# Filler products on TensorE ahead of seven waits, and twice as many behind one transpose, in a two-layer feed-forward kernel

## The chip, the cores and the metric

The kernel runs on one core of a Trainium2 chip. The metric is the device time of one execution in microseconds (us). Engines are named as in the profile: PE is TensorE (PEld its weight loads), DVE VectorE, ACT ScalarE, POOL GpSimd, SP SyncE, which here issues almost all DMAs.

## What is computed

The reference adds two feed-forward layers to x (8 sequences of 512 tokens, 256 features), each fed by a conditioning step chosen by an integer per sequence. The first layer is a quantised FFN: its input and its hidden activation h are rounded to 8 bits with one scale for the whole tensor, so nothing behind h can be quantised before the largest |h| of all tokens is known. The second layer sends each token to the best two of nine experts.

```python
def _L0_ffn_ref(x, clip_x, clip_down, w_gate, w_up, w_down):
    def _act_fake_quant(x, clip_factor):
        scale = jax.nn.sigmoid(clip_factor) * jnp.max(jnp.abs(x)) / QMAX
        return jnp.clip(_ste_round(x / scale), -QMAX - 1.0, QMAX) * scale
    ...
    h = _act_fake_quant(jax.nn.silu(gate) * up, clip_down[0])
    return jnp.einsum('bsi,hi->bsh', h, _weight_fake_quant(w_down))
...
def _L1_ffn_ref(x, Wr, Wg, Wu, Wd):
    ...
    topk_w, topk_idx = jax.lax.top_k(probs, TOP_K)
    ...
    gate = jax.nn.silu(jnp.einsum('th,ehi->tei', xf, Wg))
    hidden = gate * jnp.einsum('th,ehi->tei', xf, Wu)
    out = jnp.einsum('tei,eih,te->th', hidden, Wd, cw)
...
x = x + _L0_ffn_ref(_L0_cond_ref(x, ...), ...)
x = x + _L1_ffn_ref(_L1_cond_ref(x, ...), ...)
```

## The kernel before

The program has three stages, each one straight line of instructions.

The **front** conditions x, quantises it and computes h. Its steps are small functions (`gp`, `up` products of gate and up weights; `sl`, `st`, `uc`, `pm` activation and product; `mx` the largest |h| of a chunk, line 519 is `st`, 316 the reduction of `mx`). The text `FRONT` lists them in the order in which they are issued. A step `z_n` (lines 331 to 335) issues n matrix products of a tile of zeros, `busy`, into the PSUM bank that the next step will use; nobody reads them. There are four such banks, `wide0` to `wide3`, handed out in turn. After `FRONT` come lines 538 to 546: the largest |h| per partition (`htop_own`, line 539), a transpose on TensorE into the next bank (line 320), `z(ZEROS_BEHIND)`, that is 12 products of zeros, and then, on DVE, the maximum over all partitions and the scale of h.

The **middle** is listed in `ORDER`, again in the order of issue, one name for each piece with its batch (0 to 7) or block number. For each batch: `qa` and `qd` quantise h (ACT, then a clip on DVE), `dp` multiplies by the down weights and `dv` adds to x; `ap`, `aa`, `xp`, `xa`, `zp`, `zv` run the second conditioning step (`xs` stores x by SP), `np`, `nv`, `na`, `nw` its layer norm; `tp` transposes the normed rows back (`ta` copies them), `cp`, `ce`, `ct`, `cv`, `ca` choose the experts, `hp` and `hv` find each token's place in the expert's list, and `hg` scatters the rows into those lists in DRAM: eight indirect DMAs for each batch, on the POOL queue (line 880). `pp` and `pw` plan which blocks of 128 list rows come next.

Mixed in, and then alone in the **tail**, are blocks of 128 rows for one expert each: `R` fetches the rows, `U` and `W` the expert's weights if they change (all SP's queue), `t` transposes the rows on DVE, `g..a`, `g..b`, `g..c` are the gate and up products (line 1098), `va` to `vd` the activation, `d` the down product (line 1146), `y` the weighting and `s` the scatter into the output (POOL, line 1156). `ORDER` carries 14 blocks; the rest, up to 72, are issued by a loop.

Every engine takes its instructions in the order of issue and waits where a semaphore says so. In the middle there are six PSUM banks `bank0` to `bank5` handed out in turn, and two more, `tok0` and `tok1`, for `xp` and `zp`.

Of the kernel before, what the change touches and what calls it, by code (L numbers as in the profile page):

```python
# [32 lines left out]
P = 128  # L33
# [17 lines left out]
    up_2_3 mx_2_1 sl_2_3 up_2_4 mx_1_3 uc_2_3 up_3_0 st_2_4 gp_2_5 uc_3_0 pm_2_3 gp_3_0 mx_2_4 sl_2_5 up_2_5 up_3_1  # L51
    sl_3_0 st_2_5 gp_3_2 mx_2_5 uc_3_1 pm_3_0 mx_2_2 gp_3_1 sl_3_2 up_3_2 mx_2_3 sl_3_1 up_3_4 st_3_2 gp_3_5 pm_3_1
    uc_3_4 up_3_3 mx_3_0 sl_3_5 gp_3_4 mx_3_2 gp_3_3 sl_3_4 mx_3_1 up_3_5 sl_3_3 pm_3_4 st_3_5 st_3_3 mx_3_3 mx_3_4
    mx_3_5
"""
LAST_LOAD = "L_dT"
ZEROS_BEHIND = 12
ORDER = """
    qa0d fa1 fa0 fa2 qa0b qd0d qa0a qd0b qa0c fg0 fg1 qd0a qa2b qd0c dp0b qa1b qa1a dp0a qd1b dv0b qd1a dv0a dp1b
    qd2b qa2a xp0_1 dv1b xp0_0 ap0 xa0_1 qd2a xa0_0 dp1a qa2c xs0 aa0 qd2c qa4a zp0_0 dv1a zp0_1 zv0_0 qa3b ap1 fa3  # L60
    zv0_1 qa3a dp2a qd3b np0 aa1 qd3a dp2b dv2a pu1 pd0 nv0 dp3a dv2b na0_1 qd4a pu2 na0_0 nw0_1 xp1_1 ap2 qa4c
    xa1_1 nw0_0 xp1_0 qa4b zp1_1 dv3a xa1_0 tp0_0 pu0 aa2 zv1_1 zp1_0 ta0_0 qd4b tp0_1 qa5b zv1_0 dp3b ta0_1 qd4c
    np1 qa6b cp0 dv3b xs1 dp4b qd5b ce0 qa5a nv1 fa4 ct0 ap3 dv4b na1_1 mz0 cv0 dp4a na1_0 qa6c pd2 xp2_0 aa3 pd1
    xp2_1 nw1_1 hp0 ca0 fg2 xa2_1 hv0 tp1_1 xa2_0 zp2_1 ta1_1 xs2 nw1_0 hg0_0 zp2_0 zv2_1 tp1_0 fa5 ta1_0 zv2_0
    hg0_2 cp1 qd5a ce1 dv4a ct1 fg3 cv1 dp5b hg0_1 ap4 qd6b ca1 hp1 dv5b np2 aa4 dp5a hv1 qa6a hg0_3 nv2 pp0a qa7a
    pw0a dv5a pp0b pw0b na2_1 ap5 hg1_1 qd6a na2_0 pp0c qd6c nw2_1 dp6b qa7b hg1_3 nw2_0 xp3_1 xp3_0 xa3_1 pw0c fg4
    tp2_0 xa3_0 zp3_1 ta2_0 hg1_2 dv6b xs3 tp2_1 zv3_1 zp3_0 ta2_1 U0 qd7b cp2 aa5 zv3_0 hg1_0 ce2 fa6 dp6a qd7a
    ct2 dp7a dv6a np3 cv2 U1 dp7b W1 ap6 nv3 ca2 R0 dv7b na3_1 hp2 dv7a na3_0 xp4_0 hv2 xa4_0 xp4_1 nw3_0 R1 zp4_0
    xa4_1 zp4_1 nw3_1 tp3_0 aa6 t0 tp3_1 ta3_0 zv4_1 g0a W0 ta3_1 xs4 w0 zv4_0 fa7 cp3 va0 t1 hg2_1 g0b ce3 w1 fg5
    ct3 g0c vb0 np4 cv3 U2 g1a vc0 hg2_0 W2 nv4 g1b ca3 U3 vd0 va1 na4_1 hg2_2 g1c vb1 na4_0 nw4_1 d0 vc1 U4 hg2_3  # L70
    nw4_0 vd1 tp4_1 y0 xp5_0 ta4_1 s0 xp5_1 xa5_0 tp4_0 xa5_1 fg6 zp5_0 ta4_0 zp5_1 zv5_0 W3 cp4 zv5_1 ap7 ce4 R2
    ct4 np5 hp3 aa7 cv4 xs5 hv3 ca4 R3 nv5 hp4 hv4 na5_0 na5_1 t2 xp6_1 R4 w2 g2a xa6_1 nw5_0 nw5_1 tp5_0 va2 zp6_1
    ta5_0 t3 R5 d1 w3 zv6_1 t4 w4 tp5_1 y1 R6 xp6_0 ta5_1 s1 g2b xa6_0 zp6_0 vb2 W4 cp5 zv6_0 R7 g2c ce5 np6 g3a t5
    vc2 w5 nv6 vd2 ct5 xs6 na6_0 g3b U5 cv5 na6_1 d2 va3 fg7 hg3_3 nw6_1 ca5 nw6_0 hp5 W5 hg3_1 tp6_1 g3c hv5 ta6_1
    y2 tp6_0 vc3 U6 t6 xp7_0 hg4_0 ta6_0 w6 xp7_1 vb3 xa7_0 xa7_1 vd3 zp7_0 pp1a hg5_3 zv7_0 cp6 g4a ce6 pw1a xs7
    hg4_1 pp1b va4 g4b pw1b pp1c vb4 hg3_0 g4c pw1c d3 t7 vc4 U7 w7 hg3_2 vd4 g5a y3 W6 s2 d4 va5 hg4_3 g5b y4 W7
    s3 g5c vb5 hg4_2 g6a vc5 U8 vd5 hg5_2 g6b va6 g6c vb6 hg5_0 d5 vc6 U9 vd6 hg5_1 zp7_1 y5 ct6 W8 g7a zv7_1 s4
    cv6 d6 np7 va7 R8 nv7 ca6 na7_0 g7b s5 y6 na7_1 nw7_0 R9 hp6 g7c hv6 tp7_0 nw7_1 vc7 s6 ta7_0 R10 t8 tp7_1 w8
    g8a vb7 ta7_1 vd7 t9 d7 va8 w9 U10 R11 g8b y7 t10 s7 w10 cp7 vb8 g8c ce7 R12 ct7 g9a vc8 cv7 g9b va9 W10 t11
    ca7 U11 vd8 g9c w11 vb9 hg6_2 W9 d8 t12 vc9 w12 vd9 U12 hg6_1 g10a y8 W11 g10b s8 va10 hg6_3 g10c vb10 d9 vc10  # L80
    U13 vd10 hg6_0 g11a y9 W12 s9 d10 va11 R13 g11b y10 s10 g11c vb11 R14 g12a vc11 vd11 t13 d11 va12 w13 U14 R15
    g12b t14 y11 s11 g12c vb12 W14 hp7 vc12 R16 g13a hv7 vd12 pp2a va13 g13b pw2a R17 pp2b vb13 d12 pw2b W13 pp2c
    y12 U15 g13c pw2c s12 W15 vc13 hg7_3 U16 vd13 hg7_0 hg7_1 hg7_2
"""
BLOCKS_IN_ORDER = 14

# [2 lines left out]
def adaln_ffn_kernel(  # L89
# [21 lines left out]
    nc = tc.nc  # L111

    B, _, KC, S = xT.shape
# [21 lines left out]
    def act_scale(top, sig, name):  # L135
# [27 lines left out]
    start = rt.tile([P, NJ, E], F32, name="start")  # L163
    nc.gpsimd.iota(
        start, pattern=[[0, NJ], [CAP, E]], base=0, channel_multiplier=0, allow_small_or_imprecise_dtypes=True
# [13 lines left out]
    wdT = l0.tile([P, NM, D], BF16, name="wdT")  # L179
# [26 lines left out]
    turn_of = {}  # L206
# [35 lines left out]
    with tc.tile_pool(name="hw", bufs=1) as hw, tc.tile_pool(  # L242
# [75 lines left out]
        def across(pi, col, n, i):  # L318

            nc.tensor.transpose(pi[:, i : i + n], col.to_broadcast([n, P]), ident[:n, :n])  # L320
# [9 lines left out]
        @front  # L330
        def z(n):

            pz = wide_sb[(turn_of.get("wide", -1) + 1) % len(wide_sb)]
            for _ in range(n):
                nc.tensor.matmul(pz[:, :S], lhsT=busy[:, :P], rhs=busy, start=True, stop=True)
# [205 lines left out]
        across(ph, own, P, 0)  # L541
        z(ZEROS_BEHIND)
        htop = l0.tile([P, 1], F32, name="htop")
# [8 lines left out]
    banks_sb = [psum.tile([P, 512], F32, name=f"bank{k}") for k in range(6)]  # L552
# [615 lines left out]


    @piece  # L1170
    def pu(i, k):
        rows_of = slice(LIKELY[i] * P, (LIKELY[i] + 1) * P)
        nc.sync.dma_start(gu_sb[i].rearrange("p c n -> p (c n)"), Wx[rows_of, : KC * GU])
# [147 lines left out]
```

## Time and profile before

| | |
|---|---|
| median of 6 runs | 726.46 us (725.04 to 731.04) |
| profiled execution, its own time | 727.25 us |
| its span, first to last instruction | 725.5 us |
| mean granted TensorE clock | 0.971 |
| PE busy | 672.7 us, 93% |
| PE LDWEIGHTS busy | 569.6 us, 79% |
| DVE, ACT, POOL busy | 337.9, 202.3, 207.4 us |
| products of zeros (line 335) | 19.0 us, 55 recorded |
| longest single waits of PE | 5.3 us (line 320, for `htop_own`), 4.4 us (line 963, for `leap`), 2.8 us (line 1098, for the transposed rows) |

The page divides the span into 40 slices of 18.1 us and gives for each the busy share of every engine in tenths and the granted TensorE clock:

```profile
PE   9989798778787899999999999999999999999995
PEclk9999899898898999999999999999999999999998
DMA  8600049456377966323265532389825488225742
```

A 9 stands for 90% or more. In the fifth to the fourteenth slice (72 to 254 us) several slices have a granted clock below 0.9 and a TensorE that is idle for a tenth to three tenths of the slice; from the fifteenth on TensorE is busy for 90% or more of each slice, at a clock of 0.9 or more in all but the last. A single place is read from stretches that are cut finer than these slices, and from the instructions in order of time.

### The profile page before, as it was taken

What the parts mean: (1) busy time and instruction counts of PE and PEld (TensorE: products, weight loads), DVE (VectorE), ACT (ScalarE), POOL (GpSimd) and SP (SyncE); (2) the same over time, 40 slices, a digit from 0 to 9 for tenths busy, and PEclk for the clock granted to TensorE, in tenths of its full rate; (3) what the DMA queues carried; (4) which work ended last, traced back from release to release, by engine and by line L of the source; (5) the groups of instructions that cost most, each with busy time, mean ns of one, the idle gap of its engine ahead of it and who ended that gap; (6) DMA issues with size and microseconds to landing.
All of it is one profiled execution on the core that took longest, in us unless ns stands there. A gap on an engine that the chain in (4) does not pass through costs nothing. (4 is left out here: it accounts for less than half of the span.)

```text
span 725.5 us, 14632 instructions
## 1 busy us (share of the span) xinstructions
PE 672.7 (93%) x4678; PEld 569.6 (79%) x4688; DVE 337.9 (47%) x1036; ACT 202.3 (28%) x407; POOL 207.4 (29%) x190
## 2 busy tenths in 40 slices
PE   9989798778787899999999999999999999999995
PEld 3333254448676789899999999999999999999994
DVE  3989778674763164333333333333333333333331
ACT  4698686533330121111111111111111111111110
POOL 1036304715155535352121212212121121212212
PEclk9999899898898999999999999999999999999998
DMA  8600049456377966323265532389825488225742
GB/s 344 208 8 1 1 147 373 151 175 216 78 226 223 303 188 199 63 73 51 47 194 150 156 55 46 52 254 339 251 32 123 118 287 235 34 45 150 236 86 32
DMA packets 86641, 107.91 MB, mean 149 GB/s; under 512 B 58904, under 2 KB 75424, under 8 KB 82976
## 3 DMA queue, kind: packets, MB, share of 16 engines
q1 hardware_dynamic: 73696, 89.61, 39.6%
q0 software_dynamic: 12720, 17.31, 12.4%
q8 instruction: 39, 0.64, 0.3%
q14 instruction: 42, 0.34, 0.2%
q10 hardware_dynamic: 144, 0.01, 0.0%
HBM read 183.55 MB, written 22.83 MB: 284 GB/s over the span
## 5 line engine op out<-in xcount | busy, mean ns | idle before, releaser
L1098 PE MATMUL bank<-upper__104,lower 128*128 128x128 f32 x2636 | 316.4, 278 | 12.0 <-issue 9.1
L1098 PEld LDWEIGHTS bank<-upper__104,lower 128*128 128x128 f32 x2636 | 311.2, 194 | 17.9 <-issue 11.4
L1156 POOL DMA_INDIRECT out_dram<-upper__104,tag x67 | 104.1, 1553 | 366.7 <-DVE upper__104 L1088 281.9
L1114 DVE TENSOR_TENSOR upper__104<-bank,upper__104 128x512 f32<-128x512 f32 x67 | 46.3, 691 | 170.6 <-PE bank L1098 147.7
L1108 ACT ACTIVATE upper__104<-bank 128x512 f32<-128x512 f32 x67 | 40.1, 598 | 246.0 <-PE bank L1098 198.2
L880 POOL DMA_INDIRECT lists<-row,sloti x64 | 64.0, 1001 | 49.6 <-issue 16.9
L1146 PE MATMUL bank<-upper__104 128*128 128x256 f32 x312 | 72.4, 382 | 0.0
L1146 PEld LDWEIGHTS bank<-upper__104 128*128 128x128 f32 x312 | 58.0, 193 | 7.0
L1146 PE MATMUL tok<-upper__104 128*128 128x256 f32 x216 | 49.6, 379 | 0.0
L1146 PE MATMUL bank<-lower,upper__104 128*128 128x256 f32 x180 | 43.5, 393 | 0.2 <-issue 0.2
L1146 PEld LDWEIGHTS tok<-upper__104 128*128 128x128 f32 x216 | 39.7, 190 | 4.6
L1124 ACT ACTIVATE upper__104<-bank 128x128 f32<-128x128 f32 x41 | 11.4, 278 | 111.7 <-PE bank L1098 106.4
L1152 DVE TENSOR_SCALAR upper__104<-bank,wt 128x256 f32<-128x256 f32 x41 | 19.8, 484 | 44.6 <-PE bank L1146 40.6
L1098 PE MATMUL tok<-upper__104,lower 128*128 128x128 f32 x312 | 39.1, 275 | 0.0
L1146 PEld LDWEIGHTS bank<-lower,upper__104 128*128 128x128 f32 x180 | 34.7, 200 | 5.6 <-issue 1.1
L1098 PEld LDWEIGHTS tok<-upper__104,lower 128*128 128x128 f32 x312 | 36.9, 192 | 0.0
L1130 DVE TENSOR_TENSOR upper__104<-bank,upper__104 128x128 f32<-128x128 f32 x41 | 11.9, 290 | 43.8 <-ACT upper__104 L1125 35.8
L1124 ACT ACTIVATE upper__104<-tok 128x128 f32<-128x128 f32 x26 | 7.2, 278 | 63.9 <-PE tok L1098 63.9
L506 ACT ACTIVATE g<-wide,swg 128x1024 f32<-128x1024 f32 (+1 forms) x24 | 24.1, 1041 | 3.1 <-PE wide L482 2.4
L1152 DVE TENSOR_SCALAR upper__104<-tok,wt 128x256 f32<-128x256 f32 x26 | 12.6, 484 | 21.4 <-PE tok L1146 21.4
L640 PE MATMUL bank<-yq,wdT 128*128 128x512 bf16 x75 | 20.4, 396 | 1.9 <-ACT ha L678 1.2
L1130 DVE TENSOR_TENSOR upper__104<-tok,upper__104 128x128 f32<-128x128 f32 x26 | 7.6, 292 | 31.3 <-ACT upper__104 L1125 31.3
(215 smaller groups left out, 707.1 us busy)
## 6 DMA issues: line engine op xcount, KB each, us to landing
lower<-in_L_ffn_W_dram SPq DMA_DIRECT2D x73, 1408.0 KB
upper__104<-in_L_ffn_W_dram SPq DMA_DIRECT2D x48, 768.0 KB
lower<-in_L_ffn_W_dram SPq DMA_DIRECT2D x24, 768.0 KB
lower<-lists SPq DMA_DIRECT2D x144, 32.0 KB
upper__104<-lists SPq DMA_DIRECT2D x140, 32.0 KB
x_sb<-in_x_dram SPq DMA_DIRECT2D x8, 512.0 KB
out_dram<-xtok SPq DMA_DIRECT2D x8, 512.0 KB
lists<-pad SPq DMA_DIRECT2D x10, 130.0 KB
```

The source lines that it names most:

```text
L506: nc.scalar.activation(g, pg, AF.Silu, scale=swg[:, m : m + 1])
L640: nc.tensor.matmul(pd, lhsT=wdT[:, m, cs], rhs=hq_sb[b % 2][:, m], start=m == 0, stop=False)
L880: nc.gpsimd.indirect_dma_start(out=own_rows[(b * NJ + j) * 2 + n], out_offset=bass.IndirectOffsetOnAxis(ap=sloti_sb[b % 3][:, j, n : n + 1 ...
L1098: nc.tensor.matmul(pg[:, at * P : (at + 1) * P], lhsT=gu_sb[i % NW][:, c, n * P : (n + 1) * P], rhs=xbT_sb[i % 3][:, c], start=c == 0, sto ...
L1108: nc.scalar.activation(g_sb[i % 3][:, :4].rearrange("p m t -> p (m t)"), held.pop(("pg", i, "a")), AF.Silu)
L1114: nc.vector.tensor_tensor(hid_sb[i % 3][:, :4].rearrange("p m t -> p (m t)"), held.pop(("pg", i, "b")), g_sb[i % 3][:, :4].rearrange("p m ...
L1124: nc.scalar.activation(gs[:, 4], pg[:, :P], AF.Silu)
L1130: nc.vector.tensor_tensor(hid[:, 4], pg[:, P : 2 * P], gs[:, 4], ALU.mult)
L1146: nc.tensor.matmul(po[:, :D], lhsT=hid_sb[i % 3][:, m], rhs=dn_sb[i % NW][:, m], start=m == 0, stop=m == NM - 1)
L1152: nc.vector.tensor_scalar(y_sb[i % 3], held.pop(("po", i))[:, :D], small_["wt"][i % NX], None, ALU.mult)
L1156: nc.gpsimd.indirect_dma_start(out=out, out_offset=bass.IndirectOffsetOnAxis(ap=tag_sb[i % NX][:, 0:1].bitcast(I32), axis=0), in_=y_sb[i % 3],
```

## The change

Filler products are added at seven places, and the number behind the transpose of h's maximum goes from 12 to 24. In the front the existing step `z` is used: `z_22` at the end of `FRONT`, ahead of the transpose. In the middle a new piece `zz` issues n products of the down weights with themselves (128x512 bf16) into the bank that the next piece will take, and nothing reads them. `zz5` stands between `pp0a` and `pp0b`, `zz10` ahead of `g0a`, `zz8` ahead of `hp4`, `zz4` behind `t2` and ahead of `xp6_1`, `zz24` ahead of `tp7_0`, `zz6` ahead of `tp7_1`. Otherwise `ORDER` keeps its sequence; its lines are only broken elsewhere.

```diff
     uc_3_4 up_3_3 mx_3_0 sl_3_5 gp_3_4 mx_3_2 gp_3_3 sl_3_4 mx_3_1 up_3_5 sl_3_3 pm_3_4 st_3_5 st_3_3 mx_3_3 mx_3_4
-    mx_3_5
+    mx_3_5 z_22
 """
 LAST_LOAD = "L_dT"
-ZEROS_BEHIND = 12
+ZEROS_BEHIND = 24
 ORDER = """
...
-    ... pp0a qa7a pw0a dv5a pp0b pw0b ...
+    ... pp0a qa7a pw0a dv5a zz5 pp0b pw0b ...
-    ... tp3_1 ta3_0 zv4_1 g0a W0 ...
+    ... tp3_1 ta3_0 zv4_1 zz10 g0a W0 ...
-    ... R3 nv5 hp4 hv4 na5_0 na5_1 t2 xp6_1 ...
+    ... R3 nv5 zz8 hp4 hv4 na5_0 na5_1 t2 zz4 xp6_1 ...
-    ... hp6 g7c hv6 tp7_0 nw7_1 vc7 s6 ta7_0 R10 t8 tp7_1 ...
+    ... hp6 g7c hv6 zz24 tp7_0 nw7_1 vc7 s6 ta7_0 R10 t8 zz6 tp7_1 ...
...
     @piece
+    def zz(n, k):
+
+        pz = banks_sb[(turn_of.get("bank", -1) + 1) % len(banks_sb)]
+        for _ in range(n):
+            nc.tensor.matmul(pz, lhsT=wdT[:, 0, :P], rhs=wdT[:, :2].rearrange("p m d -> p (m d)"), start=True, stop=True)
+
+    @piece
     def pu(i, k):
```

That is 91 products more on PE: 34 with zeros and 57 with the down weights. The instructions of ACT, POOL and SP and their order stay as they are. On DVE one instruction changes its place: the memset of the small tile `half` (line 591), which stands ahead of the fourth clip of h in the kernel before, stands behind it in the changed kernel. The first product of `z_22` carries a wait for DVE, the one that frees its bank; the products of `zz` carry no wait of their own.

More of the change, by code (lines that the diff above doesn't have):

```diff
@@ L53 @@
     uc_3_4 up_3_3 mx_3_0 sl_3_5 gp_3_4 mx_3_2 gp_3_3 sl_3_4 mx_3_1 up_3_5 sl_3_3 pm_3_4 st_3_5 st_3_3 mx_3_3 mx_3_4
-    mx_3_5
+    mx_3_5 z_22
 """
 LAST_LOAD = "L_dT"
-ZEROS_BEHIND = 12
+ZEROS_BEHIND = 24
 ORDER = """
[L59 to L83, printed above, removed]
@@ new lines @@
+    qa0d fa1 fa0 fa2 qa0b qd0d qa0a qd0b qa0c fg0 fg1 qd0a qa2b qd0c dp0b qa1b qa1a dp0a qd1b dv0b qd1a dv0a dp1b qd2b
+    qa2a xp0_1 dv1b xp0_0 ap0 xa0_1 qd2a xa0_0 dp1a qa2c xs0 aa0 qd2c qa4a zp0_0 dv1a zp0_1 zv0_0 qa3b ap1 fa3 zv0_1
+    qa3a dp2a qd3b np0 aa1 qd3a dp2b dv2a pu1 pd0 nv0 dp3a dv2b na0_1 qd4a pu2 na0_0 nw0_1 xp1_1 ap2 qa4c xa1_1 nw0_0
+    xp1_0 qa4b zp1_1 dv3a xa1_0 tp0_0 pu0 aa2 zv1_1 zp1_0 ta0_0 qd4b tp0_1 qa5b zv1_0 dp3b ta0_1 qd4c np1 qa6b cp0 dv3b
+    xs1 dp4b qd5b ce0 qa5a nv1 fa4 ct0 ap3 dv4b na1_1 mz0 cv0 dp4a na1_0 qa6c pd2 xp2_0 aa3 pd1 xp2_1 nw1_1 hp0 ca0 fg2
@@ new lines @@
+    xa2_1 hv0 tp1_1 xa2_0 zp2_1 ta1_1 xs2 nw1_0 hg0_0 zp2_0 zv2_1 tp1_0 fa5 ta1_0 zv2_0 hg0_2 cp1 qd5a ce1 dv4a ct1 fg3
+    cv1 dp5b hg0_1 ap4 qd6b ca1 hp1 dv5b np2 aa4 dp5a hv1 qa6a hg0_3 nv2 pp0a qa7a pw0a dv5a zz5 pp0b pw0b na2_1 ap5
+    hg1_1 qd6a na2_0 pp0c qd6c nw2_1 dp6b qa7b hg1_3 nw2_0 xp3_1 xp3_0 xa3_1 pw0c fg4 tp2_0 xa3_0 zp3_1 ta2_0 hg1_2
+    dv6b xs3 tp2_1 zv3_1 zp3_0 ta2_1 U0 qd7b cp2 aa5 zv3_0 hg1_0 ce2 fa6 dp6a qd7a ct2 dp7a dv6a np3 cv2 U1 dp7b W1 ap6
+    nv3 ca2 R0 dv7b na3_1 hp2 dv7a na3_0 xp4_0 hv2 xa4_0 xp4_1 nw3_0 R1 zp4_0 xa4_1 zp4_1 nw3_1 tp3_0 aa6 t0 tp3_1
@@ new lines @@
+    ta3_0 zv4_1 zz10 g0a W0 ta3_1 xs4 w0 zv4_0 fa7 cp3 va0 t1 hg2_1 g0b ce3 w1 fg5 ct3 g0c vb0 np4 cv3 U2 g1a vc0 hg2_0
+    W2 nv4 g1b ca3 U3 vd0 va1 na4_1 hg2_2 g1c vb1 na4_0 nw4_1 d0 vc1 U4 hg2_3 nw4_0 vd1 tp4_1 y0 xp5_0 ta4_1 s0 xp5_1
+    xa5_0 tp4_0 xa5_1 fg6 zp5_0 ta4_0 zp5_1 zv5_0 W3 cp4 zv5_1 ap7 ce4 R2 ct4 np5 hp3 aa7 cv4 xs5 hv3 ca4 R3 nv5 zz8
+    hp4 hv4 na5_0 na5_1 t2 zz4 xp6_1 R4 w2 g2a xa6_1 nw5_0 nw5_1 tp5_0 va2 zp6_1 ta5_0 t3 R5 d1 w3 zv6_1 t4 w4 tp5_1 y1
+    R6 xp6_0 ta5_1 s1 g2b xa6_0 zp6_0 vb2 W4 cp5 zv6_0 R7 g2c ce5 np6 g3a t5 vc2 w5 nv6 vd2 ct5 xs6 na6_0 g3b U5 cv5
@@ new lines @@
+    na6_1 d2 va3 fg7 hg3_3 nw6_1 ca5 nw6_0 hp5 W5 hg3_1 tp6_1 g3c hv5 ta6_1 y2 tp6_0 vc3 U6 t6 xp7_0 hg4_0 ta6_0 w6
+    xp7_1 vb3 xa7_0 xa7_1 vd3 zp7_0 pp1a hg5_3 zv7_0 cp6 g4a ce6 pw1a xs7 hg4_1 pp1b va4 g4b pw1b pp1c vb4 hg3_0 g4c
+    pw1c d3 t7 vc4 U7 w7 hg3_2 vd4 g5a y3 W6 s2 d4 va5 hg4_3 g5b y4 W7 s3 g5c vb5 hg4_2 g6a vc5 U8 vd5 hg5_2 g6b va6
+    g6c vb6 hg5_0 d5 vc6 U9 vd6 hg5_1 zp7_1 y5 ct6 W8 g7a zv7_1 s4 cv6 d6 np7 va7 R8 nv7 ca6 na7_0 g7b s5 y6 na7_1
+    nw7_0 R9 hp6 g7c hv6 zz24 tp7_0 nw7_1 vc7 s6 ta7_0 R10 t8 zz6 tp7_1 w8 g8a vb7 ta7_1 vd7 t9 d7 va8 w9 U10 R11 g8b
@@ L84 @@
+    y7 t10 s7 w10 cp7 vb8 g8c ce7 R12 ct7 g9a vc8 cv7 g9b va9 W10 t11 ca7 U11 vd8 g9c w11 vb9 hg6_2 W9 d8 t12 vc9 w12
+    vd9 U12 hg6_1 g10a y8 W11 g10b s8 va10 hg6_3 g10c vb10 d9 vc10 U13 vd10 hg6_0 g11a y9 W12 s9 d10 va11 R13 g11b y10
+    s10 g11c vb11 R14 g12a vc11 vd11 t13 d11 va12 w13 U14 R15 g12b t14 y11 s11 g12c vb12 W14 hp7 vc12 R16 g13a hv7 vd12
+    pp2a va13 g13b pw2a R17 pp2b vb13 d12 pw2b W13 pp2c y12 U15 g13c pw2c s12 W15 vc13 hg7_3 U16 vd13 hg7_0 hg7_1 hg7_2
 """
```

## The prediction

> **What bounds the kernel now.** I read the page's 40 slices, then busy time by stretches, then TensorE's order of time with its waits, then the other engines beside each wait. From 295 us on TensorE has work without a break, so whatever time it wins or loses before that reaches the end one for one. Before 295 us it waits in many places, and a granted clock of 0.50 follows some waits. The stretches, each cut at an edge of the clock's record or at the ends of a wait (columns: stretch, length, busy us and count of PE, PEld, DVE, ACT, POOL, then granted clock, DMA share, GB/s):
>
> ```profile
> 78.40:83.73 5.33, 0.01 (x2) 0.01 (x2) 5.20 (x7) 0.75 (x1) 2.17 (x1) 0.87 0.00 0
> 82.30:89.13 6.83, 5.40 (x13) 2.04 (x14) 3.28 (x10) 4.06 (x5) 0.00 (x0) 0.50 0.00 0
> 123.26:126.67 3.41, 1.75 (x8) 0.79 (x11) 2.23 (x13) 0.27 (x1) 2.80 (x3) 1.00 1.08 372
> 130.08:133.50 3.42, 1.30 (x11) 0.66 (x11) 3.11 (x17) 3.38 (x4) 2.81 (x3) 1.00 0.42 143
> 133.50:140.33 6.83, 6.83 (x26) 4.48 (x25) 4.84 (x17) 4.46 (x8) 5.30 (x6) 0.50 0.39 131
> 160.80:164.22 3.42, 3.42 (x28) 2.78 (x28) 2.49 (x12) 0.60 (x1) 1.63 (x2) 0.50 0.71 209
> 171.04:174.46 3.42, 1.68 (x12) 1.47 (x12) 0.00 (x0) 0.00 (x0) 2.04 (x3) 1.00 0.87 216
> 184.70:188.11 3.41, 0.35 (x8) 0.20 (x6) 3.02 (x22) 1.15 (x6) 1.03 (x1) 1.00 0.66 181
> 188.11:194.94 6.83, 5.29 (x33) 5.20 (x33) 5.89 (x23) 2.83 (x6) 0.00 (x0) 0.50 0.27 46
> 295.00:705.00 410.00, 408.88 (x3069) 391.53 (x3068) 144.03 (x451) 62.42 (x164) 91.91 (x63) 1.00 0.53 135
> ```
>
> All clock edges lie on a grid of 3.41 us. A cell of it in which TensorE was busy 1.68 us or less (0.49) is followed by half clock, one with 1.75 us (0.51) is not. Half clock lasts one or two cells. Seven stretches of it stand before 295 us; the change fills waits ahead of four: 82.30, 133.50, 160.80, 188.11.
>
> TensorE's own order around the edits (start, length, line, what, count, [idle before it and what ended it]):
>
> ```profile
> 83.73 0.48 PE L320 MATMUL wide<-ident,htop_own 128*128 128x128 f32 x1 [5.32 <-DVE htop_own L539]
> 84.00 5.29 PE L335 MATMUL wide<-busy 128*128 128x512 bf16 x12
> 89.34 1.24 PE L640 MATMUL bank<-yq,wdT 128*128 128x512 bf16 x4
> ...
> 159.96 1.34 PE L1098 MATMUL bank<-upper__104,lower 128*128 128x128 f32 x8 [2.81 <-DVE upper__104 L1088]
> ...
> 262.20 1.58 PE L1098 MATMUL bank<-upper__104,lower 128*128 128x128 f32 x12
> 263.62 0.60 PE L776 MATMUL bank<-ident,row 128*128 128x128 f32 x4
> 265.25 0.63 PE L776 MATMUL bank<-ident,row 128*128 128x128 f32 x4 [1.03 <-issue]
> 265.72 1.95 PE L1098 MATMUL bank<-upper__104,lower 128*128 128x128 f32 x16
> ```
>
> The reader should see that tp7_0 at 263.62 follows g7c (262.20) with no wait at all; the largest filler, 24 products, goes between those two.
>
> Price of one filler: 8 products of the same form (L482, 128x512 bf16) take 1.89 us at full clock, so 0.216 us each; at half clock 12 take 5.29 us, so 0.43 us.
>
> **z_22 and 24 instead of 12.** The first product writes the bank that st_3_3 reads last, so it waits for the second of these two:
>
> ```profile
> 78.54 1.94 DVE L519 SCALAR_TENSOR_TENSOR upper__104<-wide,swu,g 128x512 f32<-128x512 f32 x2
> 80.52 2.94 DVE L316 TENSOR_REDUCE hmax<-upper__104 128x1 f32<-128x1024 f32 x3
> 83.49 0.18 DVE L539 TENSOR_REDUCE htop_own<-hmax 128x1 f32<-128x24 f32 x1
> ```
>
> It starts at 80.5, not at 78.4. At full clock 22 products last 4.75 us, to 85.3: the transpose that everything waits for, ready at 83.73, comes 1.6 us late; it runs 0.2 us shorter warm, +1.4. Quantisation on ACT and DVE (85.07 on) hangs on it. If 2.1 us of idle still halve the clock (edge at 82.30), 8 products run before the edge, 8 in the slow cell, 6 after: the transpose at 87.0, +3.1 net; with two slow cells +4.9. A cell must hold 1.7 of the 2.1 idle us for that, which 2.2 of 3.41 us of grid positions do; I take +3.1 and keep +1.4 and +4.9. The 12 more behind are nearly free: 24 x 0.216 = 5.2 us end about when the 12 slow ones did, counted from the transpose, and dp0b moves by the same amount. DVE's memset of half, which waits for these products and held one clip until 89.34, now stands behind that clip. No saving here: the slow stretch held only fillers nobody reads.
>
> **zz5** fits: 1.1 us against waits of 0.93 and 0.47 us around pp0b, whose reader on DVE is busy until 132.43 anyway. The cell 130.08 has 1.30 + 1.0 = 2.3 us of work, so 133.50 to 140.33 runs at full clock. dp6b then takes the 1.57 us of dp7a instead of 2.85, the two pieces of xp3 0.65 each instead of 1.1, and xp3 ends near 136.8 instead of 138.98. Behind it stand ACT's copy of xtok, SP's store of it (139.62), and in SP's queue U0, fa6, U1, W1 and the row fetch R0 (151.62) that ends the wait for g0a. So about -2.1 us, bounds 0 (SP paced by its own loads) and -2.4.
>
> **zz10** (2.2 us) fits in the 2.81 us ahead of g0a. Full clock in 160.80 to 164.22 saves 1.7 us, but I take 0 for it (bound -1.7). The reason is the next stop:
>
> ```profile
> 172.73 0.96 POOL L880 DMA_INDIRECT lists<-row,sloti  x1 [0.30 <-issue]
> 174.90 0.60 ACT L1108 ACTIVATE upper__104<-bank 128x512 f32<-128x512 f32 x1 [5.06 <-remote]
> ```
>
> ACT's silu of g1a, whose product ended at 169.35, starts at 174.90, 1.2 us after a run of Pool scatters ends (173.69). The same holds where such runs end at 212.87, 225.68, 249.10 and 290.94: readers resume 1.2 to 1.7 us later, and TensorE's instructions come singly meanwhile. That run is set by the fetch of rows, not by TensorE; coming earlier only waits longer.
>
> **zz8 and zz4** (1.7 and 0.9 us) fit in 2.24 and 1.30 us; the cell 184.70 gets 0.35 + 1.7 = 2.1 us. 188.11 to 194.94 at full clock: g2a takes 1.95 instead of 3.62 us (the rows of g2b and g2a) and xp6_1 0.6 instead of 1.12; tp5_0 then waits a little for nw5_0 (192.45 on DVE now), so d1 starts near 194.0 instead of 195.96: -2.0, bounds -1.0 (an unlucky grid leaves one slow cell) and -2.4.
>
> The Trainium skill (TensorE: Matmul & The Clock Gate, Why this matters for your kernels) names only idle gaps over about 3 us as what drops the clock. The trace differs: 188.11 went slow after gaps of 2.24 and 1.06 us. By the rule only the 5.32 us wait needed filling, the other six fillers would save nothing, and the sum below would be +8.6. I go by the rows.
>
> **zz24 and zz6.** The gap before tp7_0 is nil; its input (nw7_0 on DVE) is ready at 262.62, 1.0 us before TensorE arrives. It depends on zp7_1, which is earlier on TensorE and moves with it. So 24 x 0.216 = 5.2 us go on the path. By then nw7_1 is ready too and the 1.03 us wait before tp7_1 is gone, so zz6 (1.3 us) costs 0.3. Together +5.5; bounds +0.3 (the chain for batch 7 is late by 6 us) and +6.5 (nothing of the old wait is used up).
>
> **Sum** on the profiled 727.25 us: +3.1 - 2.1 + 0 - 2.0 + 5.5 = +4.5. The profiled run lies 0.8 above the median of 726.46, so in terms of the median 731.0. The case's own ends: +1.4 - 2.4 - 1.7 - 2.4 + 5.5 = +0.4, and +4.9 + 0 + 0 - 1.0 + 6.5 = +10.4; most of it lies from 728 to 734. 0.5% (3.6 us) is what can be told from no change: 722.8 to 730.1.
>
> **Rivals.** (1) Not slower, because zz24 is hidden: a run of Pool scatters holds up batch 7's chain, as DVE's 7.96 us of idle time before 227.40, and tp7_0 waits 5 us. Then 731.0 - 5.2 = 725.8; with a warm z_22 and zz10's saving 722.4. It decides once nw7_0 is 6.2 us later against TensorE than now (1.0 + 5.2). For it: four such holds stand elsewhere. Against: Pool's scatters stop at 248.5 and start again at 279.13, none beside this chain. (2) All clock savings come through and z_22 stays warm: the low end, 726.9. For it: the four slow stretches hold 24 us. Against: the waits behind them. (3) The fillers don't hold the clock, the grid lying otherwise: no savings, 726.46 + 3.1 + 5.5 = 735.1. For it: 0.49 and 0.51 are on different sides. Against: the filled cells reach 0.6.
>
> **How the numbers follow.** Forecast 0.62, rival 1 0.15, rival 2 0.12, rival 3 0.11. Low 725.5 leaves out the better half of rival 1, high 735 the rest of rival 3. Faster by over 0.5%: two thirds of rival 1, 0.10. Same: its rest, rival 2, and 0.18 of the forecast, 0.35. Slower: 0.55.
>
> **What would show it.** htop_own's transpose at 85 to 87 with a wait ended by TensorE's own products; full clock from 130 to 171 and 185 to 211; g0a about 2 us nearer to that transpose; a wait in g1c as long or longer; no idle time between hp6 and tp7_1, and g8a 5.5 us later against zp7_1. I am wrong if tp7_0 waits behind zz24 or if g1c's wait shrinks.

## The result, and the profile after

| | before | after |
|---|---|---|
| median | 727.45 us (49 runs, 723.36 to 739.14) | 734.84 us (23 runs, 727.36 to 740.61) |
| ratio after / before | | 1.0082, interval 1.0061 to 1.0104 |
| profiled execution, own time and span | 727.25, 725.5 us | 734.51, 732.7 us |
| mean granted TensorE clock | 0.971 | 0.978 |
| half clock between 11 and 300 us | 37.5 us | 27.3 us |

The changed kernel is slower by 6.0 us (0.61% to 1.04%), although TensorE spends 10 us less at half clock in the profiles. All ratios here leave out slow runs, those more than 1.5% above the fastest of their kernel; the two medians, of all runs, lie 7.4 us apart. Two of the 40-slice rows of the page after:

```profile
PE   9989898798856899999999999999999999999995
PEclk9999999899986999999999999999999999999998
```

The clock is now 9 in the fifth, tenth and eleventh slice, which had an 8. The new weak place is the twelfth and thirteenth slice (202 to 238 us): TensorE busy for 5 and 6 tenths, at a clock of 8 and 6. Busy time by stretches of the profile after, same columns as in the prediction:

```profile
78.52:80.65 2.13, 0.00 (x1) 0.02 (x1) 2.10 (x4) 0.74 (x1) 2.13 (x1) 1.00 0.00 0
130.24:133.80 3.56, 1.48 (x8) 0.59 (x8) 2.71 (x15) 3.16 (x4) 2.82 (x3) 1.00 0.66 137
133.80:140.60 6.80, 6.55 (x24) 3.46 (x26) 5.72 (x21) 4.08 (x7) 5.45 (x5) 0.50 0.35 116
147.39:150.90 3.51, 3.35 (x8) 1.05 (x8) 0.97 (x3) 0.10 (x1) 1.24 (x2) 0.51 0.13 31
160.80:164.22 3.42, 3.42 (x35) 2.68 (x37) 2.88 (x13) 0.20 (x1) 0.15 (x1) 1.00 0.40 111
188.40:195.00 6.60, 6.16 (x48) 5.03 (x48) 6.06 (x23) 3.48 (x7) 0.00 (x0) 1.00 0.28 45
211.94:226.51 14.57, 0.00 (x0) 0.00 (x0) 2.55 (x11) 2.01 (x6) 8.74 (x10) 0.63 0.86 298
215.70:232.80 17.10, 6.29 (x37) 5.00 (x38) 3.41 (x15) 2.47 (x6) 7.62 (x9) 0.50 0.62 212
```

Behind z_22, zz10 and zz8 with zz4 the clock stays full. Behind zz5 it does not: the same 6.8 us run at half clock, and 147.39 to 150.90 is a new such stretch. Then TensorE stands still for 14.57 us in one piece and runs at half clock until 232.80; before, the longest wait near this place was 4.35 us. TensorE in order of time, after (start, length, line, what, count, idle time before it and what ended it):

```profile
80.65 4.91 PE L334 MATMUL wide<-busy 128*128 128x512 bf16 x21 [2.13 <-DVE upper__104 L518]
85.40 0.27 PE L319 MATMUL wide<-ident,htop_own 128*128 128x128 f32 x1
85.51 5.34 PE L334 MATMUL wide<-busy 128*128 128x512 bf16 x24
...
146.39 0.63 PE L792 MATMUL bank<-zT,wr 128*32 128x128 f32 x12 [2.50 <-ACT zT L782]
...
226.51 2.08 PE L717 MATMUL tok<-w,ha 65*128 65x256 f32 x4 [14.57 <-ACT xtok L705]
...
266.01 1.58 PE L1097 MATMUL bank<-upper__104,lower 128*128 128x128 f32 x12
267.65 5.13 PE L1174 MATMUL bank<-wdT 128*128 128x512 bf16 x23
272.62 0.60 PE L775 MATMUL bank<-ident,row 128*128 128x128 f32 x4
273.05 1.46 PE L1174 MATMUL bank<-wdT 128*128 128x512 bf16 x6
274.35 0.60 PE L775 MATMUL bank<-ident,row 128*128 128x128 f32 x4
274.78 1.95 PE L1097 MATMUL bank<-upper__104,lower 128*128 128x128 f32 x16
```

The transpose of htop_own (85.40) waits for nothing but the products of z_22. zz24 (267.65) and zz6 (273.05) stand in a TensorE that has no idle time between hp6 and g8a: the whole 5.13 us is paid there. ACT in order of time around the long wait, after:

```profile
211.60 0.58 ACT L782 COPY zT<-bank 128x512 f32<-128x512 f32 x1 [4.35 <-PE tok L692]
217.40 0.28 ACT L1123 ACTIVATE upper__104<-bank 128x128 f32<-128x128 f32 x1 [5.21 <-remote]
217.70 0.27 ACT L1124 ACTIVATE upper__104<-bank 64x128 f32<-64x128 f32 x1
223.06 0.58 ACT L782 COPY zT<-bank 128x512 f32<-128x512 f32 x1 [5.09 <-remote]
225.88 1.07 ACT L705 COPY xtok<-tok 128x512 f32<-128x512 f32 x2 [2.23 <-remote]
```

The products that these instructions read ended by 211.94, yet between 212.2 and 225.8 ACT gets through three of them; "remote" means that the profile finds no engine or queue that it shows as the releaser. Meanwhile Pool issues 14 scatters of rows back to back, from 205.68 to 223.43, one each 1.27 us:

```profile
205.68 1.10 POOL L879 DMA_INDIRECT lists<-row,sloti  x1 [2.79 <-ACT row L755]
...
222.47 0.96 POOL L879 DMA_INDIRECT lists<-row,sloti  x1 [0.30 <-issue]
```

Below I call it a hold when readers resume late beside such a run. In the profile before, the same run of scatters was cut in two by 2.99 us of waiting, behind its sixth, and the hold with it:

```profile
215.86 0.96 POOL L880 DMA_INDIRECT lists<-row,sloti  x1 [2.99 <-DVE upper__104 L1152]
```

To see where time goes, each trace is cut at the first products of a few pieces. "Wait" is the start of TensorE's idle time in front of htop_own's transpose. All in us, worked out from the starts of these products:

| trace | wait to dp5b | to tp3_0 | to tp4_1 | to xp7_1 | to zp7_1 | hp6 to tp7_0 | to g8a | to g12a |
|---|---|---|---|---|---|---|---|---|
| fillers in it | z_22, 24 behind | zz5 | zz10 | zz8, zz4 | none | zz24 | zz6 | none |
| before | 46.62 | 30.22 | 23.76 | 36.51 | 39.26 | 1.70 | 2.10 | 32.60 |
| after | 47.18 | 32.44 | 20.84 | 32.36 | 47.26 | 6.88 | 2.17 | 30.89 |

Zp7_1 to hp6 is 7.14 in all traces, and from g12a to TensorE's last product these two differ by 0.6. So by xp7_1 the changed kernel had won 4.3 us against the start of the wait; the next stretch, which holds no filler, took 8.0 us back; zz24 and zz6 cost 5.25; and 1.7 us came back behind them.

### The profile page after: what moved, and what is told of

Read it like the earlier page. It is cut to its first block, busy times and chain, and to the rows that moved or that the text cites. A ratio compares the mean times of both kernels' runs of the same rounds, so it can differ in the third digit from the quotient of the medians.

```text
span 732.7 us, 14810 instructions
## 1 busy us (share of the span) xinstructions
PE 683.6 (93%) x4765; PEld 570.8 (78%) x4779; DVE 337.9 (46%) x1036; ACT 201.6 (28%) x407; POOL 206.8 (28%) x190
## 5 line engine op out<-in xcount | busy, mean ns | idle before, releaser
L1097 PEld LDWEIGHTS bank<-upper__104,lower 128*128 128x128 f32 x2636 | 307.4, 193 | 9.4 <-issue 5.7
L1097 PE MATMUL bank<-upper__104,lower 128*128 128x128 f32 x2636 | 311.0, 276 | 3.9 <-issue 3.9
L1145 PEld LDWEIGHTS bank<-lower,upper__104 128*128 128x128 f32 x180 | 33.0, 190 | 7.6 <-issue 3.8
L717 PE MATMUL tok<-w,ha 65*128 65x256 f32 x64 | 17.1, 402 | 14.6 <-ACT xtok L705 14.6
L334 PE MATMUL wide<-busy 128*128 128x512 bf16 x88 | 23.8, 425 | 3.9 <-DVE upper__104 L518 2.1
L717 PEld LDWEIGHTS tok<-w,ha 65*128 65x128 f32 x64 | 11.7, 198 | 16.5 <-ACT xtok L705 14.8
```

What stands on the lines that cost most here:

```text
L717: nc.tensor.matmul(pz[:, j * D : (j + 1) * D], lhsT=ha_sb[b % 2][:, at : at + P], rhs=batches[b]["w2"], start=False, stop=True, skip_group ...
L1097: nc.tensor.matmul(pg[:, at * P : (at + 1) * P], lhsT=gu_sb[i % NW][:, c, n * P : (n + 1) * P], rhs=xbT_sb[i % 3][:, c], start=c == 0, sto ...
L1145: nc.tensor.matmul(po[:, :D], lhsT=hid_sb[i % 3][:, m], rhs=dn_sb[i % NW][:, m], start=m == 0, stop=m == NM - 1)
```

## The experiments

Theory: zz24 and zz6 cost what they last, the middle's fillers win about what the prediction said, and the win is lost where TensorE waits for something that comes no earlier (the hold beside Pool's scatters). Rivals: the win never existed; or the front's fillers or zz24 are covered by later waits. The runs came in three sets, each beside runs of the kernel before: four where it takes 712.65 us (30 runs), four where it takes 727.14 us (32 runs; where the result was taken it was 727.45), four where it takes 712.81 us (35 runs). The sets ran on three chips, each met once; which chip gave the result is not on record. What differs is the hold: on the two chips of 713 us (sets 1 and 3), xp7_1 to zp7_1 is 26.51 us in all eight profiles, whatever the filler; where the kernel takes 727 us it is 39 to 55 us in all six. I call them chips without and with holds. The expectations were written for one kind of chip and partly met the other.

**Set 1, without holds: the parts apart.** The first leaves zz24 and zz6 out of the changed kernel, the others add one part to the kernel before.

```diff
-    ... hp6 g7c hv6 zz24 tp7_0 ... R10 t8 zz6 tp7_1 ...
+    ... hp6 g7c hv6 tp7_0 ... R10 t8 tp7_1 ...
```

> The changed kernel without zz24 and zz6; all other fillers stay. Theory: nothing covers these 30 products, since TensorE had no idle time ahead of tp7_0, so they cost 5.2 to 5.5 us (g8a came 5.24 us later against zp7_1 in the profile of the changed kernel) and this kernel is 5.2 to 5.5 us faster than the changed kernel's 734.8, near 729.5, ratio to before about 1.002. Rival: the hold ahead of zp7_0 (14.57 us in the profile after) is the cost, and the wait behind the fillers covers them; then it stays at 733 to 735, ratio 1.007 to 1.010.

Measured 712.54 us, ratio to before 1.0005 (0.9983 to 1.0026). Theory and rival were written for a kernel before of 727 us, so neither is decided; on this chip the other fillers together cost nothing that the interval shows.

```diff
-    ... hp6 g7c hv6 tp7_0 ... R10 t8 tp7_1 ...
+    ... hp6 g7c hv6 zz24 tp7_0 ... R10 t8 zz6 tp7_1 ...
```

> The kernel before with zz24 and zz6 alone. Theory: +5.2 to +5.5 us, ratio 1.0072 to 1.0076. Rival: under +2 us, if a later wait (the 1.4 us of TensorE at 290 to 292 and others like it) gives it back, ratio under 1.003.

Measured 714.35 us, 1.0025 (1.0010 to 1.0040): +1.8 us, for 6.6 us of products (5.13 and 1.46 in the profile after). That is the rival's size; the theory's +5.2 fails on this chip.

```diff
-    mx_3_5
+    mx_3_5 z_22
-ZEROS_BEHIND = 12
+ZEROS_BEHIND = 24
```

> The kernel before with z_22 and 24 in place of 12 behind the transpose alone. Theory (profile after): the clock stays full and the 22 products push the transpose late, +1.4 to +1.6 us, ratio 1.002. Rival (the prediction): 2.1 us of idle still halve the clock in most runs, +3.1 us, ratio 1.0043. Third: the full clock also helps what follows, no change or faster, ratio 0.997 to 1.000.

Measured 716.91 us, 1.0071 (1.0043 to 1.0099, 7 runs): +5.1 us, more than any of the three expected; the interval just reaches the rival's 1.0043.

```diff
-    ... dv5a pp0b ... zv4_1 g0a ... nv5 hp4 ... t2 xp6_1 ...
+    ... dv5a zz5 pp0b ... zv4_1 zz10 g0a ... nv5 zz8 hp4 ... t2 zz4 xp6_1 ...
```

> The kernel before with zz5, zz10, zz8 and zz4 alone. Theory: the sum of the changed kernel's +6.0 less 1.5 (front) less 5.3 (zz24, zz6) leaves -0.8 us, because savings of the clock are eaten by the hold of readers beside Pool's scatters: -0.5 to -1.5 us, ratio 0.998 to 0.9993. Rival 1 (the prediction): -4.1 us, ratio 0.9944. Rival 2: the fillers lengthen a hold (14.57 us ahead of zp7_0 in the profile after), slower by 1 to 3 us, ratio 1.0014 to 1.004.

Measured 713.06 us, 1.0004 (0.9981 to 1.0027): not the -4.1 us of the prediction. The times do not separate "nothing won" from "won and lost". The profiles do. TensorE in the profile with the middle's fillers alone:

```profile
235.40 1.58 PE L1097 MATMUL bank<-upper__104,lower 128*128 128x128 f32 x12
247.45 1.08 PE L775 MATMUL bank<-ident,row 128*128 128x128 f32 x4 [10.47 <-DVE place L860]
249.93 1.09 PE L775 MATMUL bank<-ident,row 128*128 128x128 f32 x4 [1.40 <-DVE row L767]
250.81 3.62 PE L1097 MATMUL bank<-upper__104,lower 128*128 128x128 f32 x16
```

TensorE starts g7c at 235.40, 26.8 us earlier than in the profile before (262.20), and then waits 10.47 us ahead of tp7_0 for the normed rows of batch 7; behind the wait g8a lasts 3.62 us in place of 1.95, at half clock. What the rows wait for is on Pool, same profile:

```profile
219.21 1.60 POOL L1155 DMA_INDIRECT out_dram<-upper__104,tag  x1 [4.28 <-DMA out_dram<-xtok]
...
228.96 1.60 POOL L1155 DMA_INDIRECT out_dram<-upper__104,tag  x1 [5.60 <-DVE upper__104 L1151]
230.87 0.97 POOL L879 DMA_INDIRECT lists<-row,sloti  x1 [0.30 <-issue]
...
241.00 1.60 POOL L1155 DMA_INDIRECT out_dram<-upper__104,tag  x1 [0.30 <-issue]
242.02 0.87 POOL L738 TENSOR_SCALAR va<-mv 128x4 f32<-128x4 f32 x1
```

The scatter s2 waits for the store of x to land, s3 (228.96) for s2, then come eight scatters of rows and s4, and only then np7 (242.02). The mean and variance that np7 reads were ready at 230.2. So tp7_0 starts at 247.45 to 252.14 in all eight profiles without holds, though hp6 starts anywhere from 235.12 to 244.12. With zz24 and zz6 alone it is the same wait, now mostly filled:

```profile
241.11 5.13 PE L1174 MATMUL bank<-wdT 128*128 128x512 bf16 x23
249.00 1.09 PE L775 MATMUL bank<-ident,row 128*128 128x128 f32 x4 [2.77 <-DVE place L860]
```

The front's fillers with a half-clock cell, in their own profile:

```profile
79.44 6.59 PE L334 MATMUL wide<-busy 128*128 128x512 bf16 x21 [2.13 <-DVE upper__104 L518]
85.87 0.27 PE L319 MATMUL wide<-ident,htop_own 128*128 128x128 f32 x1
```

22 products take 6.59 us here, 4.91 in the profile after, behind the same 2.13 us of idle time.

**Set 2, with holds.** The changed kernel again, then a change of the order on Pool meant for the chips without holds:

> The changed kernel itself, unaltered, on the chip on which the last four ran (the kernel before takes 712.7 us there, 727.5 where the result was taken). Theory: on this chip batch 7's normed rows come so late behind Pool's scatters (TensorE idles 2.8 to 11 us ahead of tp7_0 in the four profiles) that zz24 is hidden: the front's +1.5 to +3.1 is nearly all that is left, ratio 1.001 to 1.005. Rival: the parts add up as where the result was taken, +6.0 us, ratio 1.008.

Measured 731.87 us, 1.0048 (1.0014 to 1.0081), on a chip with holds after all, so the theory for a chip without was not met by it. Its profile has the same 6.88 us from hp6 to tp7_0; the idle time ahead of zp7_0 is 6.45 us.

```diff
-    ... y3 W6 s2 d4 va5 hg4_3 g5b y4 W7 s3 g5c vb5 hg4_2 ... hg5_2 g6b ... hg5_1 zp7_1 ... zv7_1 s4 cv6 d6 np7 ...
+    ... y3 W6 d4 va5 hg4_3 g5b y4 W7 g5c vb5 hg4_2 ... hg5_2 s2 g6b ... hg5_1 s3 zp7_1 ... zv7_1 cv6 d6 np7 s4 ...
```

> The kernel before with three output scatters moved in ORDER: s2 from before d4 to behind hg5_2, s3 from before g5c to behind hg5_1, s4 from before np7 to behind it; no fillers. Theory: what ends the wait ahead of tp7_0 and g8a on this chip is Pool's queue (s2 waits for the store of x to land, s3 for s2, and eight scatters of rows, s4 and np7 stand behind them), so np7 comes near 234 us instead of 243.6 and g8a 6 to 9 us earlier: 704 to 707 us, ratio 0.988 to 0.992. Rival: TensorE's own order sets the end here too; then nothing changes, ratio 0.998 to 1.002.

Measured 731.73 us, 1.0060 (1.0027 to 1.0092): slower, which neither theory nor rival had; the theory was meant for a chip without holds and was not run there. The move made a run of 20 scatters out of one of 14, and the hold grew with it: xp7_1 to zp7_1 is 52.52 us. The waits in the stretch 205 to 246 us of this kernel (what waits, total, times, longest):

```profile
ACT lgT L802 <- remote: 21.3, 1, 21.3
DVE cum L988 <- remote: 18.6, 1, 18.6
PEld bank L1097 <- issue: 13.6, 12, 2.3
PE bank L1097 <- issue: 10.6, 12, 1.3
```

TensorE gets through its products one by one, each after a pause that the profile puts down to no wait, while Pool's scatters go on (until 238.47):

```profile
226.56 0.27 PE L1097 MATMUL bank<-upper__104,lower 128*128 128x128 f32 x1 [1.25 <-issue]
229.39 0.37 PE L1097 MATMUL bank<-upper__104,lower 128*128 128x128 f32 x1 [1.04 <-issue]
...
242.81 1.44 PE L1097 MATMUL bank<-upper__104,lower 128*128 128x128 f32 x5
```

The same Pool order with the middle's fillers, and then with zz24 and zz6 as well:

```diff
-    ... dv5a pp0b ... zv4_1 g0a ... nv5 hp4 ... t2 xp6_1 ...
+    ... dv5a zz5 pp0b ... zv4_1 zz10 g0a ... nv5 zz8 hp4 ... t2 zz4 xp6_1 ...
```

> The same move of three output scatters, with zz5, zz10, zz8 and zz4. Theory: with Pool's wait gone TensorE's order sets the end, and the 4.1 us that these fillers win by hp6 (235.1 against 239.2 in the profiles of the last runs) reach it: 2 to 4 us faster than the move alone. Rival: the scatters of rows start with the fetches and are still the bound, so the fillers bring under 1 us.

Measured 733.09 us, 1.0065 (1.0037 to 1.0094): nothing gained over the Pool order alone, as the rival had it.

```diff
-    ... hp6 g7c hv6 tp7_0 ... R10 t8 tp7_1 ...
+    ... hp6 g7c hv6 zz24 tp7_0 ... R10 t8 zz6 tp7_1 ...
```

> The same as the last with zz24 and zz6 as well. Theory: with no wait ahead of tp7_0 the 30 products cost 5.2 to 5.5 us against the last kernel. Rival: still hidden, under 1.5 us.

Measured 734.91 us, 1.0093 (1.0058 to 1.0127): 0.28% more than the last, some 2 us, with intervals too wide to tell 1.5 from 5. In its profile hp6 to tp7_0 is again 6.88, against 1.70 in the two without zz24. No run on a chip with holds leaves zz24 and zz6 alone out of the changed kernel.

**Set 3, without holds: one part left out, and shorter runs on Pool.** The changed kernel without zz5, zz10, zz8 and zz4:

```diff
-    ... dv5a zz5 pp0b ... zv4_1 zz10 g0a ... nv5 zz8 hp4 ... t2 zz4 xp6_1 ...
+    ... dv5a pp0b ... zv4_1 g0a ... nv5 hp4 ... t2 xp6_1 ...
```

> The changed kernel without zz5, zz10, zz8 and zz4; the front's fillers, zz24 and zz6 stay. Theory on a chip with holds (before near 727): the four fillers win 4 us by hp6 but the holds of readers beside Pool's scatters give most of it back, so this kernel is within 2 us of the changed kernel, ratio 1.006 to 1.010. Theory on a chip without (before near 713): the wait ahead of tp7_0 gives it back, ratio 1.005 to 1.009, from the front alone. Rival: the four fillers do save 4 us, ratio 1.012 to 1.014.

Measured 714.71 us, 1.0019 (0.9993 to 1.0045), below the 1.005 to 1.009 of the theory for a chip without holds. The changed kernel without z_22 and with 12 behind the transpose:

```diff
-    mx_3_5 z_22
+    mx_3_5
-ZEROS_BEHIND = 24
+ZEROS_BEHIND = 12
```

> The changed kernel without z_22 and with 12 in place of 24 behind the transpose; zz5, zz10, zz8, zz4, zz24 and zz6 stay. Theory: the front's fillers cost 1.5 us where the clock stays full and 3.1 where one cell goes slow (profiles so far: +1.45, +1.45 and +3.1 from the start of TensorE's wait to dp0b), so this kernel is 1.5 to 3.1 us faster than the changed one; ratio 1.002 to 1.006 on a chip with holds, 1.000 to 1.003 on one without. Rival: the front costs nothing by the end, ratio as the changed kernel's, 1.005 to 1.008.

Measured 711.92 us, 0.9989 (0.9972 to 1.0006), a little under the range expected and well under the rival's. The kernel before with six scatters moved:

```diff
-    ... xs7 hg4_1 pp1b ... vb4 hg3_0 g4c ... w7 hg3_2 vd4 g5a y3 W6 s2 d4 ...
+    ... xs7 pp1b ... vb4 g4c ... w7 vd4 g5a y3 W6 s2 hg4_1 hg3_0 hg3_2 d4 ...
```

> The kernel before with six scatters of rows (hg4_1, hg3_0, hg3_2) moved on Pool behind the output scatter s2, so that 14 back to back become 8, s2, 8, s3, 8; no fillers. Theory on a chip with holds: a hold begins 4.5 to 6.5 us into a run of scatters and ends 1.2 to 1.7 us behind it (24 in a row held TensorE until 241), so the holds ahead of zp7_0 and pp1c shrink from some 7 to 10 us to under 4: 3 to 6 us faster, ratio 0.992 to 0.996. Theory on a chip without: s2 no longer waits behind 14 scatters, np7 and R8's rows come some 5 us earlier: ratio 0.992 to 0.996. Rival: the order on Pool decides nothing, ratio 0.998 to 1.002.

Measured 713.29 us, 1.0007 (0.9989 to 1.0025). The rival holds. Pool in its profile:

```profile
208.94 0.96 POOL L879 DMA_INDIRECT lists<-row,sloti  x1 [0.30 <-issue]
219.23 1.60 POOL L1155 DMA_INDIRECT out_dram<-upper__104,tag  x1 [9.33 <-DMA out_dram<-xtok]
...
231.29 1.60 POOL L1155 DMA_INDIRECT out_dram<-upper__104,tag  x1 [0.30 <-issue]
```

With eight scatters in place of 14, Pool is free 7.5 us earlier (209.9 against 217.4 in the kernel with zz24 and zz6 alone), and s2 still comes at 219.2, against 221.6: it waits for the store of x, which SP issued at 206.85, behind three loads of weights that SP had issued since 200.38. So not the run on Pool ahead of it but that store sets s2. The run tells less of np7 and tp7_0: the six moved scatters now stand between s2 and s3, and s3 (231.29) comes 12.1 us behind s2, against 8.9 with zz24 and zz6 alone. That the store is slow because it lands behind the weights was not tried. What shorter runs do on a chip with holds was not tried either: this set met a chip without.

The same move with zz5, zz10, zz8 and zz4, put in as above:

> The same move of six scatters, with zz5, zz10, zz8 and zz4. Theory: with less held or waited for ahead of tp7_0, more of the 4.1 us of these fillers reaches the end: 1 to 4 us faster than the move alone. Rival: none of it does.

Measured 712.02 us, 1.0002 (0.9982 to 1.0022): nothing gained over the move alone, as the rival had it. No version beats the kernel before beyond its interval.

The stretches of all these profiles, as above:

| profile | wait to dp5b | to tp3_0 | to tp4_1 | to xp7_1 | to zp7_1 | hp6 to tp7_0 | to g8a | to g12a |
|---|---|---|---|---|---|---|---|---|
| with holds | | | | | | | | |
| e5, changed | 47.19 | 31.39 | 20.81 | 33.61 | 43.32 | 6.88 | 2.17 | 30.89 |
| e6, Pool order | 46.55 | 30.09 | 23.08 | 34.40 | 52.52 | 1.70 | 2.12 | 31.84 |
| e7, and middle | 45.87 | 33.90 | 22.29 | 33.77 | 47.78 | 1.70 | 2.10 | 32.36 |
| e8, and zz24, zz6 | 45.82 | 32.34 | 21.31 | 32.32 | 55.21 | 6.88 | 2.17 | 30.89 |
| without holds | | | | | | | | |
| e1, front and middle | 47.15 | 25.36 | 19.14 | 33.73 | 26.51 | 12.83 | 3.37 | 32.16 |
| e2, zz24, zz6 | 45.80 | 26.35 | 21.87 | 34.45 | 26.51 | 9.81 | 3.64 | 30.89 |
| e3, front | 48.85 | 27.84 | 21.79 | 34.69 | 26.51 | 5.04 | 3.37 | 34.66 |
| e4, middle | 45.79 | 25.35 | 20.83 | 32.33 | 26.51 | 12.33 | 3.36 | 32.74 |
| e9, front, zz24, zz6 | 47.15 | 27.83 | 21.61 | 34.74 | 26.51 | 8.74 | 2.95 | 32.06 |
| e10, middle, zz24, zz6 | 45.79 | 25.31 | 19.22 | 33.65 | 26.51 | 14.90 | 4.06 | 30.89 |
| e11, shorter runs | 45.80 | 26.32 | 21.75 | 34.23 | 26.51 | 10.78 | 3.37 | 33.40 |
| e12, and middle | 45.80 | 25.34 | 21.18 | 32.32 | 26.51 | 12.17 | 3.37 | 32.36 |

## Why the prediction was right, and where its steps were not

The forecast was +4.5 us and 731.0; measured +6.0 (4.4 to 7.6; a median of 734.84) and, in the second set, +3.5 (1.0 to 5.9). The direction and the main cost, zz24 and zz6, are right. But against the profile before, four of the five terms were off by 2.2 to 4.3 us, and one stretch that the sum left alone moved by 4 to 8.

| term | predicted | after against before | what the other profiles show |
|---|---|---|---|
| z_22, 24 behind | +3.1 (+1.4, +4.9) | +0.6 | 47.15 to 47.19 in four, 48.85 in one, against 45.8 in seven without |
| zz5 | -2.1 | +2.2 | without holds -1.7 (-2.5 beside z_22, -1.0 without it), with holds +2.4 |
| zz10 | 0 (-1.7) | -2.9 | without holds -1.7, with holds -2.1 |
| zz8, zz4 | -2.0 | -4.2 | without holds -1.5, with holds -1.4 against e6 |
| xp7_1 to zp7_1 | 0 | +8.0 | e5 +4.1 |
| zz24, zz6 | +5.5 | +5.25 | e5 and e8 the same, to 0.01 |
| behind g8a | 0 | -1.7 | 30.89 in five of six with zz24, 31.84 to 34.66 without |

(The last column compares the means of the profiles with the filler and without it on the same kind of chip. The -4.2 of zz8 and zz4 has 2.1 us in it that the profile before lost to a hold in g3c, which lasted 3.43 us there and 1.34 after.)

**z_22: the mechanism was right, the term mis-sized.** Both ends that the prediction kept were seen: +1.35 with a full clock (47.15 against 45.80) and +3.05 with one slow cell (48.85). I took the worse one for likely because 2.2 of 3.41 us of positions should bring it; it came once in five profiles. Against the profile before it is only +0.6, because before itself spent 0.8 more than seven of the eight others without z_22. The Trainium skill (TensorE: Matmul & The Clock Gate, What's actually happening) says that the activity window runs freely, without regard to the kernel's start; the five profiles agree, since 2.13 us of idle time at the same place was followed by half clock in one and not in four. The line that the prediction drew between 0.49 and 0.51 of a cell is not sharp: in e1 the cell from 78.69 to 82.10 was busy for 1.68 us (0.49) and full clock followed.

**zz5: the step that failed.** "The cell 130.08 has 1.30 + 1.0 = 2.3 us of work, so 133.50 to 140.33 runs at full clock" is borne out without holds: all four profiles with zz5 run at full clock there. With holds only e8 does; e5 and e7 have one slow cell there and the profile after has two, because the wait ahead of pp0a had grown from 1.21 to 1.85 us and left that cell 1.48 us of work in 3.56. In all four with zz5 TensorE then met one wait of 2.4 to 3.9 us between 137.7 and 146.4 (the 2.50 us ahead of 146.39 above) and the clock fell there; the two without zz5 had 2.2 and 1.9 us of waits in that place, and no half clock behind them before 150. So the time that zz5 won was given back a few us later, in a longer wait and a new slow stretch; what makes that wait longer was not shown. The sign that the prediction gave for this saving, g0a some 2 us nearer to htop_own's transpose, did not come: 76.2 us before, 76.6 after. Where nothing holds, the terms are borne out in the main, and against a rule: the Trainium skill (TensorE: Matmul & The Clock Gate, Why this matters for your kernels) warns in that section of gaps over about 3 us only, but filling shorter waits (zz5, zz8 and zz4) won 1.7 and 1.5 us there. In the stretch of zz8 and zz4 half clock went from 6.83 us in each of the four profiles without them to 3.41 or none in the four with them.

**zz10: "I take 0 for it" was wrong.** The prediction held that a hold in g1c would absorb the saving, and named the sign against that: "if g1c's wait shrinks". It did: g1c to d0 took 4.02 us before and 1.34 after; a wait of 0.35 and one of 1.05 us moved into d0. A saving of 1.7 to 2.1 us comes through as far as tp4_1 on both kinds of chip.

**The sum of the middle was nearly right, its way to the end was not.** Zz5, zz10, zz8 and zz4 were to bring 4.1 us. From dp5b to xp7_1 it is 4.9 us after against before, and 4.9 without holds (78.4 against 83.4, means of four). None of it shows in the times of the middle's fillers alone (on the chip without holds the interval leaves room for 1.4 us). With holds, Pool's run of 14 scatters begins 127.1 to 127.2 us behind the wait in both profiles of the changed kernel and 126.8 before: it came no earlier though TensorE did. TensorE then stood beside it, in the profile after until 3.1 us behind its end, in e5 until 5.0 us before its end. Without holds the wait ahead of tp7_0 takes the win. This is the rule that the prediction applied to zz10 ("coming earlier only waits longer"); it belonged to the next hold, where no term of the sum stood.

**zz24 and zz6 were right on the chip of the result and not a law.** TensorE had no idle time ahead of tp7_0, and 5.13 us of products cost 5.18. Behind it 0.9 to 1.7 us come back by g12a: the wait of 1.4 us in g11a at 290 us, which the prediction did not count, is gone. The reading that Pool issues no scatter from 248.5 to 279.13 left out three output scatters (258.68, 264.12 and 271.06); TensorE waited for none of them ahead of tp7_0. Rival 1, given 0.15, is what the two other chips show: tp7_0 waits 3.2 to 11.0 us without zz24 there and 1.7 to 7.9 us behind it. The way is near the one it named: np7 stands in Pool's queue behind s2, which waits for the store of x, and then behind s3, eight scatters of rows and s4. That the whole change would cost little there is likely from the parts; it was not run there.

So +4.5 came near the measured +6.0 in part by luck. In these two profiles the front cost 2.5 us less than forecast, zz10, zz8 and zz4 won 5.1 us more, and 1.7 us came back behind g8a; against that stand zz5, 4.3 us worse, and 8.0 us lost from xp7_1 to zp7_1 that were in no term.

What stays open: whether the 14.57 us ahead of zp7_0 are caused by the change or are one draw of a hold that varies (6.45 us in the second profile of the same kernel); what a hold is, and why one chip has them and two have not; and why the front's fillers cost 5.1 us alone (e3) but nothing that the intervals show beside other parts (e1 against e4, e9 against e2). A part of that is seen: without zz5, dp5b to tp3_0 takes 27.8 us behind the front's fillers (e3, e9) and 26.3 without them (e2, e11).

## What to carry to other kernels

A filler that fits a wait can keep the clock, but what it wins ends at the next thing that TensorE does not set; find that thing, here a run of scatters on Pool and a store that lands late, before counting the win. A filler in front of an instruction whose input is ready costs what it lasts (5.18 us here for 5.13 of products), and one profile can't tell that the input will be ready elsewhere: the same place had no wait on one chip and up to 11 us on another. Time a change on more than one chip when the kernel before differs between them by more than the change is worth.

## What the runs showed of the hardware

The same kernel took 727.14 us on one chip and 712.65 and 712.81 on two others. The kernel before was profiled only where the result was taken; its nearest profile without holds is e11. Of the two, before takes 12.75 us more from xp7_1 to zp7_1 (39.26 against 26.51) and 9.0 more from the wait to xp7_1, and e11 gives 9.1 of that back ahead of tp7_0 (10.78 against 1.70); Pool issues its scatters every 1.27 us in both. During a hold ACT and DVE resume products' results late (up to 21.3 us, e6), and TensorE's own instructions come 0.7 to 1.4 us apart with no wait named. The stretch lengthens with the scatters in a row: 39.26 us with a run cut into 6 and 8 (before), 47.78 with 6 and 14 (e7), 43.32 and 47.26 with 14 (e5, after), 52.52 and 55.21 with 20 (e6, e8). That the order of s2 and s3 itself adds to the last three was not separated. A hold costs twice, as a wait and by the half clock that follows it: 54.6 us of half clock by 300 us in e6, against 37.5 in e11, neither with fillers in the middle.
